# Conv, scan, attention and experts on one core: first scans with their C products on GpSimd, later openings by chunks, side work in halves

## The chip, the cores and the metric

The kernel runs on one core of a Trainium2 chip. The metric is the device time of one execution in microseconds. The engines are TensorE (PE), VectorE (DVE), ScalarE (ACT), GpSimd (POOL) and SyncE (SP), which here only issues DMAs.

## The reference, cut

There are 4 images of L = 4096 tokens with 128 channels, all in fp32. Each image goes through two layers. Layer 0 makes three selective scans of its tokens: forward, backward, and in 16 interleaved slices. Layer 1 is an attention with 16 heads of 8 features, a small feed-forward block, and 64 experts that each pool the tokens.

```python
# layer 0, for each of three orders of the tokens ("order" 0, 1, 2)
xz = in_proj_w @ norm(x)                      # 512 x L: 256 rows x, 256 rows z
u = silu(causal_conv1d(x, conv_w, conv_b))    # 4 taps
dt_raw, B, C = split(x_proj_w @ u)            # 8, 16 and 16 rows
delta = softplus(dt_w @ dt_raw + dt_b)        # 256 x L
h[d, n] = h[d, n] * exp(delta[d] * A[d, n]) + delta[d] * u[d] * B[n]    # over t
y[d] = sum_n h[d, n] * C[n] + D[d] * u[d]
out = out_proj_w @ ((y_f + y_b + y_s) * silu(z)) + x
# layer 1
q = ring(norm(out) + theta)                   # products of cosines, 16 heads x 8
ctx = softmax(q q^T / sqrt(8)) q              # 4096 x 4096 for each head and image
x1 = ln(norm(out) + w_comb @ ctx); h = relu(w1 @ z(x1)); x2 = ln(x1 + w2 @ h)
# experts: gate logits over tokens, best 8 of each, pooled tokens through two matrices, scattered back
```

## The kernel before

**Scan layout.** A scan step treats 8 channels x 16 states as rows: 128 partitions by T = 1024 tokens. A chunk (an order's 1024 tokens, 4 to an order) needs 32 steps, written as (order, c, k, j) with k in 0..7 and j in 0..3. An image has 3 x 4 x 32 = 384 steps. `Scans.of_image` is a generator that emits one step in two yields. `load` (L489) brings `delta` and `du` from DRAM, spread over 8 states each, for two steps at a time. `exp` (L503) makes dA = exp(delta * A) on ACT. `inputs` (L510) multiplies du by B on DVE. `step` scans on DVE (L519), copies the last column to `ends` on POOL (L521), calls `inputs` for the next step, and multiplies h by C on DVE (L524). `total` (L551) sums over the states with matmuls against `sel`. `out` (L567) adds D * u once for four steps and stores the result (L570, L576, L580) from POOL's queue. `product` (L544) makes `du` of a later chunk in parts between steps.

**Inputs.** `Inputs.pieces` yields the pieces that make the scans' inputs for all images: `norm`, `slices`, `of_chunk` (convolution as matmuls L387, silu L394, projections L401 and copy L404, L418, softplus L422, stores L370, L406, L407) and `gate` (silu of z, L351). They go through `flow`, which keeps two pieces in hand and steps them in turn, the second starting 10 yields after the first. Three PSUM tiles of 1024 columns are theirs.

**Stages.** An order of instructions written by hand sets all of this: each engine's queue gets its instructions in the order in which the generators yield. `Pace.run(share)` advances a chain of generators by a share of a step for each call.

1. First scans: image 0's 384 steps beside all images' inputs, 1.03 yields of the inputs for each yield of the scan.
2. `block.opening(0)`: tokens of image 0 (sum of the three orders' results, times silu(z), output projection, norm) and their rings q and v.
3. Loops over images 0, 1, 2. A loop has 1024 rounds of (j, qb, kc): 4 matmuls of scores (L924), two ACT exponentials of 128x1024 (L929, tile e), 4 matmuls of values into `acc` (L938). After each round, `beside(i)` advances the next image's scans and one step of other work: `after` of the image before (feed-forward), then `opening` of the next image, which starts when the next image's scans are done. What is left of the opening when the loop ends runs by itself before the next loop.
4. The loop over image 3. Its blocks of 512 queries are finished in turn, so that `after` of image 3 and the experts' pooling run beside it, 0.92 steps a round. A `yield PE` from `bank.take` marks a step that is about to put matmuls on PE; the side work has one PSUM bank.
5. The end: the last block's feed-forward, expert matrices, scatter.

In a round the order is scores of the next round, values of this one, then what stands beside it:

```python
            if i + 1 < len(rounds):
                scores(i + 1)
            values(i)
            if kc == NT - 1:
                sums(j, qb, i)          # acc copied by ACT, L947
            ...
            beside(i)
```

The side work's matmuls are `co` (L1041), `zt` (L1062), `h` (L1076), `fo` (L1087), `xT` (L1109), `lg` (L1119), `wt` (L1254), `pool` (L1265).

Of the kernel before, what the change touches and what calls it, by code (L numbers as in the profile page):

```python
# [16 lines left out]
P = 128  # L17
# [6 lines left out]
SLICES = 16  # L24
T = 1024
# [183 lines left out]

def early(b, order, c):  # L210

    return b == 0 or (b == 1 and order == 0 and c < 2)
# [15 lines left out]
class Inputs:  # L228
# [26 lines left out]
    def bank(self, name):  # L255
        while self.held == 3:
            yield WAIT
        self.held += 1
        return self.ps.tile([P, T], F32, tag="a", name=name)
# [4 lines left out]
    def pieces(self, images):  # L264

        for b in images:
            self.sz[b] = self.dram.tile([DI, L], F32, name=f"d_sz_{b}")
            yield self.norm(b)
            for order in range(3):
                if order == 2:  # L270
                    yield self.slices(b)
                for c in range(NC):
                    yield self.of_chunk(b, order, c)
                    third, at = divmod(order * NC + c, 3)
                    if at == 2:
                        yield self.gate(b, third)

    def norm(self, b):
# [10 lines left out]
        for g in range(NC):  # L289
            x_g = self.piece.tile([P, 8, C], F32, tag="x_g", bufs=2, name=f"x_{b}_{g}")  # L290
            nc.sync.dma_start(out=x_g, in_=xin[:, g * 8 : g * 8 + 8, :])
            yield
            ps = yield from self.bank(f"xt_{b}_{g}")
            for k in range(8):
                nc.tensor.transpose(ps[:, k * P : (k + 1) * P], x_g[:, k, :], self.ident)
            cut = xn[:, 3 + g * T : 3 + (g + 1) * T]
            nc.scalar.copy(cut, ps)
            self.leave()
            yield
            for k in range(2):  # L300
                nc.vector.bn_stats(stats[:, 2 * g + k, :], cut[:, k * 512 : (k + 1) * 512])
# [36 lines left out]
    def gate(self, b, g):  # L338
        nc, xn = self.nc, self.normed[b]
        s_g = self.piece.tile([P, 2, T], F32, tag="u", bufs=2, name=f"z_{b}_{g}")  # L340
        for m in range(2):
            ps = yield from self.bank(f"z_{b}_{g}_{m}")
            for i in range(T // 512):
                at = 3 + g * T + i * 512
                nc.tensor.matmul(
                    ps[:, i * 512 : (i + 1) * 512], self.w_z[:, m * P : (m + 1) * P], xn[:, at : at + 512],
                    start=True, stop=True,
                )
            yield
            yield  # L350
            nc.scalar.activation(s_g[:, m, :], ps, AF.Silu)  # L351
            self.leave()
        nc.gpsimd.dma_start(out=self.sz[b].rearrange("(m p) t -> p m t", p=P)[:, :, g * T : (g + 1) * T], in_=s_g)
# [3 lines left out]
    def of_chunk(self, b, order, c):  # L357
# [11 lines left out]
        def keep(name, t):  # L369
            nc.gpsimd.dma_start(out=made[name].rearrange("(m p) t -> p m t", p=P), in_=t)  # L370
# [11 lines left out]
        banks = []  # L382
        for m in range(2):
            ps = yield from self.bank(f"cv_{key}_{m}")
            for g, cut in enumerate(halves):
                for k in range(4):
                    nc.tensor.matmul(  # L387
                        ps[:, cut], w["conv"][:, k, m * P : (m + 1) * P], reads(k, g), start=(k == 0), stop=(k == 3)
                    )
                yield  # L390
            banks.append(ps)
        yield
        for m in range(2):
            nc.scalar.activation(u[:, m, :], banks[m], AF.Silu, bias=w["conv_b"][:, m : m + 1])  # L394
# [3 lines left out]
        ps = yield from self.bank(f"xd_{key}")  # L398
        for cut in halves:
            for m in range(2):  # L400
                nc.tensor.matmul(ps[:X_ROWS, cut], w["x"][:, m, :], u[:, m, cut], start=(m == 0), stop=(m == 1))  # L401
        yield
        xd = self.piece.tile([X_ROWS, T], F32, tag="xd", name=f"xds_{key}")
        nc.scalar.copy(xd, ps[:X_ROWS])  # L404
        self.leave()
        nc.gpsimd.dma_start(out=made["bc"][0], in_=xd[B_ROW : B_ROW + NS])  # L406
        nc.gpsimd.dma_start(out=made["bc"][1], in_=xd[C_ROW : C_ROW + NS])  # L407
        yield

        r = self.piece.tile([P, 2, T], F32, tag="r", bufs=2, name=f"r_{key}")  # L410
        banks = []
        for m in range(2):
            banks.append((yield from self.bank(f"dt_{key}_{m}")))
        for m in range(2):
# [1156 lines left out]
```

## Time and profile before

| | us |
|---|---|
| runs | 11714.78, 11721.87, 11722.49 |
| median | 11721.87 |
| the profiled execution, its own time | 11713.44 |
| its span, first to last instruction | 11711.7 |
| first scans (from the first scan's inputs to the last scan of image 0) | 97 to 1955 |
| opening of image 0 | 1955 to 2176 |
| loops over images 0, 1, 2 | 2176 to 4571, 4615 to 6978, 7021 to 9346 |
| loop over image 3 | 9348 to 11463 |
| end | 11463 to 11712 |

Busy time over the span: PE 10319 us (88%), ACT 10020 (86%), DVE 8551 (73%), POOL 3373 (29%). These are means over stages that differ, so they tell little; the stages have to be read one by one. In the profile a line such as L519 is the line of the kernel, a tile's name stands without its buffer number, and `out<-in` names what an instruction writes and reads. An idle time is put down to what ended it.

### The profile page before, as it was taken

To read this page: it belongs to the slowest core of one execution; us is meant where nothing else is said; L and a number is where in the kernel's file an instruction comes from. 1 tells how busy PE (TensorE), PEld (TensorE's weight loads), DVE (VectorE), ACT (ScalarE), POOL (GpSimd) and SP (SyncE) were. 2 spreads that over 40 slices of the span, in tenths; PEclk is the share of its full clock that TensorE was granted. 3 is DMA by queue.
4 is the path that set the end of the run, shared out by engine and by line. 5 is a ranking of instruction groups with operands and counts; after the bars stand their busy time and mean duration, and the time that the engine had idled before them with its cause. 6 is when DMAs were issued, how large, how long until landed. Compare 5 with 4: busy or idle time off the path is not lost.

```text
span 11711.7 us, 181745 instructions
## 1 busy us (share of the span) xinstructions
PE 10319.3 (88%) x68038; PEld 3430.9 (29%) x68038; DVE 8550.7 (73%) x8743; ACT 10019.7 (86%) x10604; POOL 3373.1 (29%) x4017
## 2 busy tenths in 40 slices
PE   6677674699999997999999979999999999999995
PEld 2222231222222232333333222333332223333323
DVE  7999998898988877998898879989887321101113
ACT  4565563699999997999999989999999999999992
POOL 5525362231323222324244223243341111000011
PEclk8888786799999998999999989999999999999997
DMA  6777777655565556665656566565555322222125
GB/s 186 219 222 209 212 209 204 174 152 154 150 155 147 145 161 173 158 157 147 156 140 154 150 176 168 152 153 142 150 138 137 120 93 67 75 70 76 59 73 187
DMA packets 835819, 1747.47 MB, mean 149 GB/s; under 512 B 141070, under 2 KB 373574, under 8 KB 834678
## 3 DMA queue, kind: packets, MB, share of 16 engines
q1 hardware_dynamic: 649438, 1318.65, 42.3%
q0 software_dynamic: 144000, 307.48, 8.5%
q10 hardware_dynamic: 41496, 109.71, 3.5%
q8 instruction: 534, 8.75, 0.3%
q14 instruction: 351, 2.88, 0.1%
HBM read 1379.76 MB, written 355.47 MB: 148 GB/s over the span
## 4 chain that ended last, share of the span: by engine, by line
PE 58%; DVE 13%; ACT 10%; issue 9%; DMA 8%; SPq 1%; POOL 0%; ACTq 0%; DVEq 0%; POOLq 0%
PE acc L938 33%; PE s L924 15%; ACT e L929 7%; DVE h L519 7%; PE y L551 4%; DMA delta<-d_delta 3%; DVE dB L510 2%; DMA du<-d_du 1%; PE fo L1087 1%; DVE du L510 1%; PE h L1076 1%; DMA y<-d_y 1%; PE cv L387 1%; DMA w<-in_L_ffn_weight_dram 1%; ACT dA L503 1%
## 5 line engine op out<-in xcount | busy, mean ns | idle before, releaser
L929 ACT ACTIVATE e<-s 128x1024 f32<-128x1024 f32 x8192 | 7777.3, 1102 | 357.9 <-PE s L924 313.0
L938 PE MATMUL acc<-e,val 128*32 128x512 f32 x32768 | 5676.3, 612 | 79.5 <-ACT av L947 78.7
L924 PE MATMUL s<-qm,key 32*128 32x512 f32 x16384 | 2784.7, 501 | 370.5 <-ACT e L929 310.5
L521 POOL COPY ends<-h 128x1 f32<-128x1 f32 x1152 | 1608.5, 1396 | 2597.6 <-DVE h L519 2590.9
L924 PEld LDWEIGHTS s<-qm,key 32*128 32x128 f32 x16384 | 1067.4, 183 | 3619.9 <-issue 1948.1
L938 PEld LDWEIGHTS acc<-e,val 128*32 128x32 f32 x32768 | 1028.4, 108 | 2009.7 <-issue 1015.4
L519 DVE TENSOR_TENSOR_SCAN h<-delta,ends,du 128x1024 f32<-128x1024 f32 x576 | 1353.5, 2350 | 86.3 <-ACT delta L503 77.1
L519 DVE TENSOR_TENSOR_SCAN h<-dA,ends,dB 128x1024 f32<-128x1024 f32 x576 | 1353.3, 2350 | 21.4 <-ACT dA L503 17.8
L503 ACT ACTIVATE dA<-delta,A 128x1024 f32<-128x1024 f32 x768 | 938.6, 1222 | 482.0 <-DMA delta<-d_delta 426.4
L510 DVE TENSOR_TENSOR dB<-du,B 128x1024 f32<-128x1024 f32 x768 | 931.8, 1213 | 549.8 <-PE y L551 370.1
L503 ACT ACTIVATE delta<-delta,A 128x1024 f32<-128x1024 f32 x768 | 938.9, 1222 | 75.3 <-PE y L551 68.4
L510 DVE TENSOR_TENSOR du<-du,B 128x1024 f32<-128x1024 f32 x768 | 925.6, 1205 | 28.7 <-DMA B<-d_bc 28.7
L524 DVE TENSOR_TENSOR dB<-h,C 128x1024 f32<-128x1024 f32 x768 | 939.6, 1223 | 0.0
L524 DVE TENSOR_TENSOR du<-h,C 128x1024 f32<-128x1024 f32 x768 | 939.4, 1223 | 0.1
L551 PE MATMUL y<-du,sel 128*32 128x256 f32 x6144 | 738.5, 404 | 184.1 <-DVE du L524 183.9
L551 PE MATMUL y<-dB,sel 128*32 128x256 f32 x6144 | 733.5, 400 | 91.6 <-DVE dB L524 40.9
L953 POOL DMA_DIRECT2D d_ctx<-av x512 | 260.7, 521 | 922.5 <-ACT av L947 912.7
L387 PE MATMUL cv<-xn,conv 128*128 128x512 f32 x1024 | 488.4, 632 | 20.0 <-DVE xn L322 20.0
L580 POOL DMA_DIRECT2D d_y<-o x512 | 329.6, 673 | 550.8 <-DVE o L567 489.9
L545 POOL DMA_DIRECT2D d_du<-x_delta x272 | 155.2, 571 | 1105.4 <-DVE x_delta L544 1029.2
L519 DVE TENSOR_TENSOR_SCAN h<-delta,du 128x1024 f32<-128x1024 f32 x192 | 439.2, 2287 | 13.1 <-ACT delta L503 7.1
L519 DVE TENSOR_TENSOR_SCAN h<-dA,dB 128x1024 f32<-128x1024 f32 x192 | 439.2, 2287 | 11.9 <-ACT dA L503 10.6
(245 smaller groups left out, 6450.8 us busy)
## 6 DMA issues: line engine op xcount, KB each, us to landing
delta<-d_delta SPq DMA_DIRECT2D x768, 512.0 KB
du<-d_du SPq DMA_DIRECT2D x576, 512.0 KB
du<-d_du ACTq DMA_DIRECT2D x192, 512.0 KB
key<-d_q SPq DMA_DIRECT2D x352, 256.0 KB
d_u<-u POOLq DMA_DIRECT2D x48, 1024.0 KB, 7.1
d_delta<-r POOLq DMA_DIRECT2D x48, 1024.0 KB, 6.5
B<-d_bc SPq DMA_DIRECT2D x96, 512.0 KB
C<-d_bc SPq DMA_DIRECT2D x96, 512.0 KB
```

What stands on the lines that cost most here:

```text
L387: nc.tensor.matmul(ps[:, cut], w["conv"][:, k, m * P : (m + 1) * P], reads(k, g), start=(k == 0), stop=(k == 3))
L503: nc.scalar.activation(tiles["delta", s], t, AF.Exp, scale=A)
L510: nc.vector.tensor_mul(tiles["du", s], du, spread[order, c, "B", j % 2])
L519: nc.vector.tensor_tensor_scan(h, dA, dB, first, ALU.mult, ALU.add)
L521: nc.gpsimd.tensor_copy(ends[order, c][:, at : at + 1], h[:, T - 1 :])
L524: nc.vector.tensor_mul(dB, h, spread[order, c, "C", j % 2])
L551: nc.tensor.matmul(y[32 * g : 32 * g + 32, : T // 4], self.sel[:, j // 2, :], hC[:, 256 * g : 256 * g + 256], start=(j == 0), stop=(j == 3),)
L580: nc.gpsimd.dma_start(out=to.rearrange("p (i j) -> p i j", i=SLICES)[:, :, at : at + n], in_=rows.rearrange("p (i j) -> p i j", i=SLICES),)
L924: nc.tensor.matmul(s_ps[:, k, :], keys[f"{i // 4}"][rows, cut].bitcast(F32R), queries[j, qb][rows, :].bitcast(F32R), start=True, stop=True,)
L929: nc.scalar.activation(e, s_ps, AF.Exp, scale=1.0 / math.sqrt(D))
L938: nc.tensor.matmul(accs[j, qb][32 * k : 32 * k + 32, :], v[:, k * VW : k * VW + 32], es[i][k // 2][:, k % 2, :], start=(kc == 0), stop=(kc ...
L953: nc.gpsimd.dma_start(out=self.context[b][h * D : h * D + D, cut], in_=av[32 * k : 32 * k + D, :])
```

## The change

**First scans.** Each `step` of image 0 (`alone`) multiplies h by C on POOL, into tiles of their own (hC, 5 of them), and DVE multiplies by B two steps ahead instead of one, always into a `dB` tile. `exp` writes dA to PSUM (two tiles of 1024 columns); the `h` of odd steps takes the buffers that dA had. Loads go out 4 steps ahead instead of 2. The sums' stores are kept for later and issued from SP. The inputs use PSUM tiles of 512 columns (three of them): every convolution, projection, silu and softplus is done by halves, silu one half at a time. The stores of the inputs go out from SP's queue instead of POOL's. The du products of the 14 early chunks (12 of image 0, 2 of image 1) move from DVE to POOL, two halves each, except the first chunk's. The inputs advance by 1.2 yields instead of 1.03.

**Later images.** Images 1 to 3 scan the orders as 1, 2, 0. Order 0's result stands in a DRAM tensor for each chunk. A block of `tokens` waits until the sums that it reads are stored, and the opening runs as soon as `after` is done, before the scans have ended. The scans aim at round 890 instead of 860.

**Loops.** In each round `beside(i)` comes before `values(i)`. In the last loop `acc` is copied by DVE, the matmul pieces zt, h, fo, xT and lg are cut in two by a `yield PE`, and side work goes by `Pace.turn(1.5, free)`: at most one PE step in a round, none in every third round up to round 830.

```diff
 def early(b, order, c):
-    return b == 0 or (b == 1 and order == 0 and c < 2)
+    return b == 0 or (b == 1 and order == orders(b)[0] and c < 2)
...
+        return self.ps.tile([P, 512], F32, tag="a", name=name)
...
         def keep(name, t):
-            nc.gpsimd.dma_start(out=made[name].rearrange("(m p) t -> p m t", p=P), in_=t)
+            nc.sync.dma_start(out=made[name].rearrange("(m p) t -> p m t", p=P), in_=t)
...
+                ps = yield from self.bank(f"cv_{key}_{m}_{g}")
                 for k in range(4):
                     nc.tensor.matmul(
+                        ps, w["conv"][:, k, m * P : (m + 1) * P], reads(k, g), start=(k == 0), stop=(k == 3)
                     )
                 yield
+                nc.scalar.activation(u[:, m, cut], ps, AF.Silu, bias=bias)
+                self.leave()
...
+            yield
+            for g, cut in enumerate(halves):
+                nc.scalar.activation(
+                    r[:, m, cut], banks[g], AF.Softplus, bias=w["dt_proj_b"][:, m : m + 1]
+                )
+                self.leave()
...
+            by = nc.vector if (b, order, c) == (0, orders(0)[0], 0) else nc.gpsimd
+            for m in range(2):
+                by.tensor_mul(u[:, m, :], r[:, m, :], u[:, m, :])
...
+            if alone:
+                tiles["delta", s] = self.ps.tile([P, T], F32, tag="dA", name=f"dA_{b}_{s}")
...
+            tag = "dA" if alone and j % 2 else "h"
+            h = self.deep.tile([P, T], F32, tag=tag, bufs=2, name=f"h_{b}_{s}")
             first = 0.0 if c == 0 else ends[order, c - 1][:, at : at + 1]
             nc.vector.tensor_tensor_scan(h, dA, dB, first, ALU.mult, ALU.add)
             if c < NC - 1:
                 nc.gpsimd.tensor_copy(ends[order, c][:, at : at + 1], h[:, T - 1 :])
+            if alone:
+                if s + 2 < n:
+                    inputs(s + 2)
+                tiles["du", s] = self.lone.tile([P, T], F32, tag="hC", bufs=5, name=f"hC_{b}_{s}")
+                nc.gpsimd.tensor_mul(tiles["du", s], h, spread[order, c, "C", j % 2])
+                return
...
+        c, part = divmod(g, T // 512)
+        while self.scans.stored[b] < min(8 * (2 * NC + c + 1) + 2, 8 * 3 * NC):
+            yield WAIT
...
-            nc.scalar.copy(av, accs.pop((j, qb)))
+            (nc.vector.tensor_copy if by_block else nc.scalar.copy)(av, accs.pop((j, qb)))
...
-            values(i)
-            if kc == NT - 1:
-                sums(j, qb, i)
...
             beside(i)
+            values(i)
+            if kc == NT - 1:
+                sums(j, qb, i)
...
                 for f in range(4):
+                    if f == 2:
+                        yield from self.pause()
...
+    def turn(self, share, free):
+        self.credit = min(self.credit + share, 3.0)
+        while self.credit >= 1 and not self.done and (free or self.then is not PE):
+            free = free and self.then is not PE
+            self.step()
...
-                others.run(1.03)
+                others.run(1.2)
...
-                following.run(min(1.3, max(0.5, left / max(1, 860 - i))))
-                other = last if not last.done else opens if left == 0.0 else None
-                if other is None:
+                following.run(min(1.3, max(0.5, left / max(1, 890 - i))))
+                other = opens if last.done else last
+                if other.done:
                     return
...
-        block.loop(nb - 1, lambda i: last.run(0.92), True)
+        block.loop(nb - 1, lambda i: last.turn(1.5, i % 3 > 0 or i > 830), True)
```

## The prediction

> **What bounds the kernel now.** I first cut the span at its stages (busy time by stretch; columns: length, then PE, PEld, DVE, ACT, POOL busy with counts, then granted clock, DMA share, GB/s).
>
> ```profile
> 97.00:1955.00 1858.00, 1319.65 (x5558) 504.57 (x5558) 1827.88 (x1331) 1082.85 (x935) 915.79 (x819) 0.82 0.74 214
> ...
> 2176.00:4571.00 2395.00, 2224.45 (x15726) 693.22 (x15726) 2058.77 (x1729) 2326.78 (x2495) 678.36 (x897) 0.98 0.59 153
> 4571.00:4615.00 44.00, 7.83 (x52) 3.39 (x50) 36.35 (x47) 6.74 (x8) 15.28 (x15) 0.62 0.74 222
> ...
> 9348.00:11463.00 2115.00, 2074.01 (x13534) 651.67 (x13534) 361.83 (x942) 1940.32 (x2110) 174.77 (x307) 0.99 0.24 73
> ```
>
> The first scans (384 steps in 1858 us, 4.84 each) are bound by DVE, busy 1828. The loops over images 0 to 2 (2395, 2363, 2325 us) are bound by ACT, 97% busy. Between them lie 44 and 43 us in which ACT does almost nothing. In the last loop ACT idles 175 of 2115 us.
>
> Next the timeline inside the first stage, DVE's and then POOL's (start, length):
>
> ```profile
> 1009.16 1.20 DVE L510 TENSOR_TENSOR du<-du,B 128x1024 f32<-128x1024 f32 x1
> 1010.28 1.22 DVE L524 TENSOR_TENSOR dB<-h,C 128x1024 f32<-128x1024 f32 x1
> 1011.41 2.35 DVE L519 TENSOR_TENSOR_SCAN h<-delta,ends,du 128x1024 f32<-128x1024 f32 x1
> 1013.68 1.20 DVE L510 TENSOR_TENSOR dB<-du,B 128x1024 f32<-128x1024 f32 x1
> ```
> ```profile
> 1009.31 2.23 POOL L521 COPY ends<-h 128x1 f32<-128x1 f32 x1 [5.20 <-DVE h L519]
> ```
>
> By starts a step costs DVE 1.12 (times B) + 1.13 (times C) + 2.27 (scan). POOL's copy of one column starts at 1009.31 and ends at 1011.54, just after the two products: it was locked out. The same shows on a POOL operation that takes 0.19 us undisturbed (minimum, median, maximum ns):
>
> ```profile
> L48 POOL TENSOR_TENSOR rs_x<-mv_x,eps x24: 195/2144/2158, 4754.5 to 6333.7; 128x4 f32<-128x4 f32 x24
> ```
>
> The long ones began under a scan of two SBUF tensors. ACT has 775 us left in this stage, but look at its table loads (groups by form, the stage's window):
>
> ```profile
> L503 ACT ACT_TABLE_LOAD x127 | 162.9, 1283 | 98.3 <-DMA delta<-d_delta 96.6
> ...
> L394 ACT ACT_TABLE_LOAD x47 | 60.3, 1283 | 0.8
> L422 ACT ACT_TABLE_LOAD x47 | 60.3, 1283 | 0.8
> ...
> L351 ACT ACT_TABLE_LOAD x32 | 41.1, 1283 | 0.6
> ```
>
> Last, the waits of 4571 to 4615, and ACT's of the last loop:
>
> ```profile
> ACT e L929 <- PE s L924: 18.2, 1, 18.2
> ...
> PE s L924 <- DMA key<-d_q: 15.2, 1, 15.2
> ```
> ```profile
> ACT e L929 <- PE s L924: 135.0, 188, 1.1
> ACT e L929 <- PE h L1076: 39.2, 60, 0.7
> ```
>
> The gap is the next image's opening, whose end the first keys await. In the last loop ACT waits for scores that stand behind side matmuls on PE.
>
> **What the Trainium skill says.** "SBUF — State Buffer", Who interferes with whom: a DVE instruction with two SBUF inputs and a GpSimd instruction that reads SBUF lock each other out whole; one with at most one SBUF input doesn't. The trace agrees: under scans L48 takes about 2.15 us, but under L1079 (one PSUM tensor and a column from SBUF) 192 to 197 ns. "GPSIMD Engine Reference", Elementwise: a product of 2048 fp32 takes 4497 ns on GpSimd against 2293 on DVE. DVE's 128x2048 product takes 2302 here; the trace has no GpSimd product of that kind. "ScalarE: Activation LUTs", What ACT_TABLE_LOAD costs: 1283 ns and a drain of some 1380. The trace has the 1283, but only 17 ns before and 12 after it; with the lost overlap (about 0.1) I price a switch at 1.41.
>
> **Part 1, the first scans.** The products with C go to POOL: 384 x 1.13 = 434 us off DVE. The scan reads dA from PSUM; that operand should cost DVE nothing (a 128x256 sum with a PSUM operand, L776, takes 417 ns; L544 from SBUF 420), at worst 0.1 a step. POOL's product I take at 2.25 (half of the page's 4497); bounds are 1.13 (DVE's own) and, an estimate, 3.4 (half as much again). The lock then sets the chain: after a scan DVE multiplies by B (1.12) while POOL waits; then POOL copies (0.04 + 0.19) and multiplies (2.25) while the next scan runs (2.27), and the next B product waits for POOL. That makes 3.6 a step. At every fourth step the sum L567 (0.5) makes it 3.9, on average 3.67; x384 = 1409. The du products of 13 early chunks also go to POOL: 26 x 2.25 = 59. Sum 1468, 3.82 a step. POOL is freed of the stage's stores (about 510 issues, 312 us busy), which go to SP. SP then issues some 870 DMAs at about 0.54 = 470 us, and each store waits there for ACT or DVE with the next loads queued behind it; since loads go out four steps ahead (15 us) I cost that at nothing. The same DMA traffic in 1680 us is a share of 0.74 x 1858/1680 = 0.82, which the trace reaches in places.
>
> ACT is what may eat the gain. In 512-column pieces each silu half comes after a yield of its own and each softplus pair too, so exponentials fall between them. Following the yields of the two interleaved chunks and the scan step by step, before gives 255 loads (the page has 127+48+48+32) and after gives 460: 139 before silu of u, 61 softplus, 31 gates, 229 exponentials. ACT's work by spacing: exponentials 384 x 1.05 = 403, silu and softplus 384 halves x 0.585 (1.012 less 512 x 0.833 ns) = 225, copies 128 x 0.47 = 60, gates 64 x 0.51 = 33, slices 30, loads 460 x 1.41 = 649: 1400 us, nearly all in the first 353 steps (at pace 1.2 the inputs end there), 3.87 a step. That is the chain's own pace, and it is uneven: stretches with silus need 5 to 6.5, and with two dA buffers ACT can be only one step ahead. Adding up the larger of chain (3.82) and ACT's work gives about 1570 if four steps may balance, 1690 if none may. PE's waits for POOL's products and ACT's for half a convolution speak for the upper end: I take 1680, **a gain of 180**; bounds +30 (slower) and -290. The input banks shrink from three of 1024 columns to three of 512, so PE can lead ACT by three halves only; that wait is in the choice of the upper end.
>
> **Part 2, loops 0 to 2.** With order 0 scanned last, opening blocks start at 74 of 96 stored sums, and only two blocks and the second half's rings are left when the scans end near round 900 of 1024. At about a step a round that is 60 rounds: the opening ends inside the loop. The gaps (87 us) go, less the 9 us of exponentials done there and a few: -75. Values after the side work lets PE fill its wait for the last e of a round; PE-caused idle is 39, 39 and 56 us per loop: -30. DVE (86% and 87% busy in the first two loops) gets crowded while opening and scans overlap: +15. **-90**, bounds 0 and -190. Costed at nothing: the swapped order and order 0's sums in a tensor per chunk (the same bytes), the pace of 890 in place of 860 (124 rounds are left behind it), and the wait for stored sums at the head of an opening block, behind which nothing is queued, since it only skips its turn.
>
> **Part 3, the last loop.** Rounds without side matmuls start 1.815 us apart. By what PE did between, the others cost extra: 60 with fo 1.05 each, 60 with h 0.84, 30 with co 0.64, 48 with wt or pool 1.03, 15 with zt 0.47, 14 each with lg 0.97 and xT 0.57: 211 us. That is more than the pieces themselves (fo and h 0.86), for they stand between the values, which end late, and the next scores. After, 404 pieces of at most 0.43 stand between scores and values, where PE waits for e anyway, one in a round and none in every third. In 1.81 us PE needs 0.44 for scores and 0.9 for values, so a half nearly fits; I take 0.2 each (bounds 0 and 0.35): 81, a gain of 130. The 31 accumulator copies that cost a round 0.47 move to a DVE that is 17% busy, but PE still waits for them: -7. By the yields the side work now ends near round 951 instead of 13 steps after the loop: -12. **-150**, bounds -70 and -220.
>
> **Sum.** The profiled execution took 11713.4 (span 11711.7, 1.7 around it): 11713 - 180 - 90 - 150 = 11293. The median of the runs is 8 above that execution: **11300**.
>
> **Rivals.** (a) ACT takes the whole gain of part 1: for it the 205 added loads (289 us), against it ACT's 775 idle us; 11722 - 240 = 11480. (b) The loops give little, because DVE saturates in the overlap and a PE half costs its switch again: 0 and -70 for parts 2 and 3; 11722 - 180 - 70 = 11470. (c) Slower: the scan still locks POOL out, because its first state is a column in SBUF. Then nothing overlaps: 1.12 + 2.27 + 0.23 + 2.25 = 5.87 a step, 384 x 5.87 + 59 = 2313, +455; 11722 + 455 - 240 = 11940. It decides from 5.47 us a step (4.84 + 240/384). Against it: L1079 and L567 also read such columns, and POOL ran under them undisturbed. (d) The PSUM decays don't buy a faster stage because POOL's product takes over 3.4: part 1 is 0, as in (a).
>
> **Numbers.** The forecast 0.69, (a) with (d) 0.17, (b) 0.08, slower by (c) or a like lock 0.05, nothing measurable 0.01. A measurement of this kernel tells 0.2% (23 us) from no change. Range 11130 (stage 1 at 1570, and 60 more from the loops) to 11530 (past (a) and (b), with 50 for what both can lose besides); it leaves out (c) and the best corner.
>
> **What would show it.** Right: first stage 1570 to 1750 us, 4.1 to 4.6 a step, POOL above DVE in busy share, about 460 table loads, POOL's products near 2.3; no stretch over 10 us without e between the loops; last loop under 2000 and no e waiting for h. Wrong: scans or B products of 3 us and more (a lock that I misread), POOL's product far from 2.3, a first stage near 1850 with ACT over 85% busy, or the opening still running when a loop ends.

## The result

The changed kernel takes 11545.6 us (median of 4 runs, 11534.4 to 11551.4) against 11721.3 before: a ratio of 0.985, with a 95% interval of 0.9833 to 0.9867. It is faster by 176 us, or 1.5%, which is clear of the noise; the forecast was 420, and the time lies 16 us above the range. The profiled execution spans 11538.0 us. I cut it at the same places as before: first scan to last scan of image 0, then the loops from first to last exponential e.

| us | before | predicted change | after | change |
|---|---|---|---|---|
| up to the first scan | 101.6 | 0 | 113.8 | +12 |
| first scans (384 steps) | 1834.7 | -180 | 1828.2 | **-7** |
| to the first e | 239.3 | 0 | 243.9 | +5 |
| loops 0 to 2 | 7083.9 | -15 | 7063.9 | -20 |
| the two gaps between them | 86.9 | -75 | 6.3 | -81 |
| last loop | 2114.8 | -138 | 2030.8 | **-84** |
| after it | 248.9 | -12 | 249.4 | 0 |

The sum of the last column is the 174 us between the two spans (the remaining stretch before the last loop is 1.6 us in both). Part 2 came as worked out. Part 1 gave nothing, part 3 some 60%. A single execution of the loops over images 0 to 2 tells little below some 10 us: in the runs below that leave them alone they take 7060 to 7083 us, 7071 on average.

Busy time by stretch of the kernel after; columns as before (length, PE, PEld, DVE, ACT, POOL busy with counts, then clock, DMA share, GB/s):

```profile
110.00:1945.00 1835.00, 1421.40 (x5527) 556.60 (x5531) 1432.67 (x926) 1376.44 (x1409) 1339.81 (x714) 0.82 0.75 213
2186.00:4563.00 2377.00, 2128.59 (x15690) 631.62 (x15690) 2043.14 (x1740) 2321.89 (x2490) 682.93 (x907) 0.98 0.60 156
4563.00:4564.20 1.20, 1.20 (x10) 0.29 (x6) 1.20 (x2) 0.48 (x2) 0.00 (x0) 1.00 0.93 252
9258.00:11289.00 2031.00, 1961.69 (x13688) 630.76 (x13690) 393.39 (x995) 1924.51 (x2078) 177.11 (x314) 0.98 0.25 76
```

In the first row DVE lost 395 us of work and the stretch is nearly as long as it was. Four engines are now busy for 73 to 78% each and none of them is full: the stage changed from one that DVE filled into one in which every engine waits. The third row is all that is left of the first gap.

A step of the first scans in the timeline of the kernel after (start, length, engine, line):

```profile
999.12 2.35 DVE L542 TENSOR_TENSOR_SCAN h<-dA,ends,dB 128x1024 f32<-128x1024 f32 x1 [7.19 <-issue]
...
1001.38 1.20 DVE L532 TENSOR_TENSOR dB<-du,B 128x1024 f32<-128x1024 f32 x1
1001.53 1.09 POOL L544 COPY ends<-h 128x1 f32<-128x1 f32 x1 [7.25 <-DVE h L542]
...
1002.58 2.35 POOL L549 TENSOR_TENSOR hC<-h,C 128x1024 f32<-128x1024 f32 x1
...
1003.55 2.35 DVE L542 TENSOR_TENSOR_SCAN h<-dA,ends,dB 128x1024 f32<-128x1024 f32 x1 [0.97 <-POOL ends L544]
```

POOL's copy waits out the product with B, its product takes 2.35 us and runs beside the scan: the mechanism is the one predicted, and a scan that reads dA from PSUM costs DVE no more than before (2.35). The first line shows the trouble: DVE stood idle for 7.19 us before that scan. The profile puts this down to "issue", that is, to nothing that it could name; but the exponential dA that the scan reads ended at 999.03, 0.09 us before it. Over the stage the distance from scan to scan is about 3.4 us or less in a quarter of the steps, 4.4 in the middle one, and over 6.8 in one of ten; before, the middle half lay between 4.51 and 4.90.

ACT's table loads in the stage (groups by form; count, busy us, mean ns, idle before):

```profile
L525 ACT ACT_TABLE_LOAD x228 | 292.5, 1283 | 23.8 <-DMA delta<-d_delta 11.5 <-DMA du<-d_du 4.4 <-DMA d_y<-o 3.7
L400 ACT ACT_TABLE_LOAD x136 | 174.5, 1283 | 69.7 <-PE cv L396 49.2 <-issue 16.4 <-DMA d_du<-u 2.0
...
L427 ACT ACT_TABLE_LOAD x60 | 77.0, 1283 | 3.1 <-issue 2.1
...
L358 ACT ACT_TABLE_LOAD x31 | 39.8, 1283 | 0.6
```

They are 455 in this window and 461 in all, where 460 were counted from the turns.

### The profile page after: what moved, and what is told of

It reads as the page before. It is cut to its first block, busy times and chain, and to the rows that moved or that the text cites. A ratio compares the mean times of both kernels' runs of the same rounds, so it can differ in the third digit from the quotient of the medians.

```text
span 11538.0 us, 182909 instructions
## 1 busy us (share of the span) xinstructions
PE 10009.7 (87%) x68358; PEld 3314.4 (29%) x68358; DVE 8174.7 (71%) x8379; ACT 10305.7 (89%) x11065; POOL 3770.4 (33%) x3917
## 4 chain that ended last, share of the span: by engine, by line
PE 34%; ACT 23%; issue 14%; DVE 7%; DMA 6%; POOL 1%; SPq 1%; ACTq 0%; DVEq 0%; POOLq 0%
PE acc L992 20%; ACT e L983 20%; PE s L978 9%; DVE h L542 2%; DMA du<-d_du 1%; DMA delta<-d_delta 1%; ACT dA L525 1%; PE fo L1149 1%; ACT delta L525 1%; PE h L1136 1%; DMA w<-in_L_ffn_weight_dram 1%; DVE dB L532 1%; PE y L580 1%; DMA y<-d_y 0%; DVE du L553 0%
## 5 line engine op out<-in xcount | busy, mean ns | idle before, releaser
L992 PE MATMUL acc<-e,val 128*32 128x512 f32 x32768 | 5250.0, 616 | 105.5 <-ACT av L1001 91.6
L544 POOL COPY ends<-h 128x1 f32<-128x1 f32 x1152 | 1264.9, 1099 | 2501.6 <-DVE h L542 2486.2
L542 DVE TENSOR_TENSOR_SCAN h<-dA,ends,dB 128x1024 f32<-128x1024 f32 x720 | 1687.6, 2344 | 337.2 <-issue 205.7
L532 DVE TENSOR_TENSOR dB<-du,B 128x1024 f32<-128x1024 f32 x960 | 1197.0, 1247 | 408.0 <-PE y L580 221.2
L542 DVE TENSOR_TENSOR_SCAN h<-delta,ends,du 128x1024 f32<-128x1024 f32 x432 | 1012.1, 2343 | 132.1 <-ACT delta L525 65.4
L549 POOL TENSOR_TENSOR hC<-h,C 128x1024 f32<-128x1024 f32 x384 | 976.8, 2544 | 146.8 <-DVE h L542 73.0
L553 DVE TENSOR_TENSOR du<-h,C 128x1024 f32<-128x1024 f32 x576 | 700.9, 1217 | 0.1
L553 DVE TENSOR_TENSOR dB<-h,C 128x1024 f32<-128x1024 f32 x576 | 700.8, 1217 | 0.0
L580 PE MATMUL y<-dB,sel 128*32 128x256 f32 x4608 | 376.7, 399 | 9.9 <-DVE xT L1176 6.2
L580 PE MATMUL y<-hC,sel 128*32 128x256 f32 x3072 | 255.5, 467 | 144.7 <-DVE o L596 139.6
```

Of the source, the lines that this page charges most:

```text
L532: nc.vector.tensor_mul(tiles["du", s], du, spread[order, c, "B", j % 2])
L542: nc.vector.tensor_tensor_scan(h, dA, dB, first, ALU.mult, ALU.add)
L544: nc.gpsimd.tensor_copy(ends[order, c][:, at : at + 1], h[:, T - 1 :])
L549: nc.gpsimd.tensor_mul(tiles["du", s], h, spread[order, c, "C", j % 2])
L553: nc.vector.tensor_mul(dB, h, spread[order, c, "C", j % 2])
L580: nc.tensor.matmul(y[32 * g : 32 * g + 32, : T // 4], self.sel[:, j // 2, :], hC[:, 256 * g : 256 * g + 256], start=(j == 0), stop=(j == 3),)
```

## What DVE waits for: the first stage

**Where the idle time is.** For every step I took from the trace whether DVE was idle before the scan (by more than 0.15 us) and whether the exponential dA had only just ended. Before the change this happened at the very first scan alone. After it, 193 of 384 scans start late behind their exponential, and DVE idles 337.5 us there. The stretch that ends in the 7.19 us, on PE and ACT:

```profile
987.89 1.28 ACT L400 ACT_TABLE_LOAD   x1 [3.50 <-PE cv L396]
...
988.74 10.57 PE L396 MATMUL cv<-xn,conv 128*128 128x512 f32 x24
...
992.48 0.69 ACT L400 ACTIVATE u<-cv,conv_b 128x512 f32<-128x512 f32 x1 [2.61 <-PE cv L396]
995.91 0.69 ACT L400 ACTIVATE u<-cv,conv_b 128x512 f32<-128x512 f32 x1 [2.75 <-PE cv L396]
...
996.62 1.28 ACT L525 ACT_TABLE_LOAD   x1
997.91 1.12 ACT L525 ACTIVATE dA<-delta,A 128x1024 f32<-128x1024 f32 x1
```

ACT takes its work in order. It waits for half a convolution, does its silu, waits for the next half; PE needs 3.43 us for each. Then it loads the exponential's table, and only then comes the exponential that the scan has been waiting for since about 992. Two PSUM buffers of dA let ACT be one step ahead, so little of this can be done earlier. (A third buffer was not tried.) In the 193 late steps, between the moment when the buffer came free and the start of the exponential, ACT spent 600 us on table loads (377 of them for the exponential itself), and some 170 in waits for convolutions, 125 in silus and 120 in softplus.

**Theory.** Three things stand between the chain (3.6 us a step) and the stage: table loads, dense convolutions on PE with ACT waiting between the halves, and what PE has to wait for in its order. **Rivals:** the loads are all of it; or they are nothing and POOL's part is simply too slow. In the table, stage is first to last scan of image 0, gap from there to the first e; these come from one profile of each kernel. The totals of the changed kernel and of e3 are medians of 4 executions, the others are a single one. The runs e4 and e8 further down leave the stage alone and show it at 1829.5 and 1833.3, so some 5 us in it mean nothing.

| run | stage | gap | last loop | total |
|---|---|---|---|---|
| after | 1828 | 244 | 2031 | 11545.6 |
| e1 no table loads | 1697 | 245 | 2029 | 11407.7 |
| e2 decays in SBUF | 2213 | 246 | 2032 | 11936.5 |
| e3 silus in pairs | 1807 | 245 | 2032 | 11529.5 |
| e5 C products on DVE | 1937 | 247 | 2035 | 11666.0 |
| e6 sum one step earlier | 1777 | 242 | 2032 | 11493.5 |
| e12 two taps | 1736 | 244 | 2031 | 11456.8 |
| e7 = e1 + two taps | 1590 | 246 | 2032 | 11313.5 |
| e9 = e7 + e6 | 1561 | 244 | 2038 | 11278.0 |
| e13 = e9 + new loads of x | 1487 | 273 | 2035 | 11224.4 |

**e1, no table loads.** Silu and softplus are replaced by exponentials, so these two functions are left out.

```diff
-   nc.scalar.activation(u[:, m, cut], ps, AF.Silu, bias=bias)
+   nc.scalar.activation(u[:, m, cut], ps, AF.Exp, bias=bias)
```
The same for z and for r.

> The changed kernel with silu and softplus of the scans' inputs computed as exponentials, so that the first scans need no table load (the scans then work on other numbers; every shape and every order of instructions is kept). The changed kernel needs 1828 us from the first scan to the last one of image 0. Theory A (the exponential that the next scan needs stands on ACT behind table loads, with only one step of lead): the 460 loads become one or two, and the stage falls to the chain of B product, column copy and POOL's C product, 3.6 to 3.9 us a step: 1400 to 1520 us, the run some 300 to 400 us under the changed kernel. Theory B (PE and ACT wait for each other over the three half banks, whatever the tables do): the stage stays over 1720. Theory C (the shared port between DVE and POOL sets the pace): the stage stays over 1750.

The stage falls by 131 us to 1697, between the theories. The idle time behind late exponentials falls from 337.5 to 149.6 us, but ACT's waits for convolutions rise. Waits between 110 and 1700 us (total, times, longest), first of the kernel after, then of e1:

```profile
ACT u L400 <- PE cv L396: 93.3, 50, 4.7
```
```profile
ACT u L400 <- PE cv L396: 435.7, 159, 12.1
...
PE y L580 <- DVE o L596: 69.4, 21, 7.3
```

Freed of 584 us of loads (455 x 1.283), ACT waits 342 us longer for PE before its silus (a part of this wait stood before the loads themselves until now, 49.2 us in the stage). So all loads together are worth 131, and PE's share is next.

**e2, decays in SBUF.** The exponentials of image 0 go to SBUF as before, so that h has its two buffers of before again, and all else stays.

```diff
-   if alone:
-       tiles["delta", s] = self.ps.tile([P, T], F32, tag="dA", name=f"dA_{b}_{s}")
-   elif j % 2 == 0:
+   if j % 2 == 0:
        tiles["delta", s] = self.deep.tile([P, T], F32, tag="dA", bufs=2, name=f"dA_{b}_{s}")
    ...
-   tag = "dA" if alone and j % 2 else "h"
-   h = self.deep.tile([P, T], F32, tag=tag, bufs=2, name=f"h_{b}_{s}")
+   h = self.deep.tile([P, T], F32, tag="h", bufs=2, name=f"h_{b}_{s}")
```

> The changed kernel with dA written to SBUF as in the kernel before (even steps in a buffer, odd steps in place of delta), C products still on POOL. The scan then has two SBUF inputs. If a scan of two SBUF inputs locks POOL's product out for its whole length, nothing overlaps: 1.12 + 2.27 + 0.23 + 2.3 = 5.9 us a step, the stage 2250 to 2320 us, 400 to 500 over the changed kernel. If POOL's product only shares bandwidth with the scan, or is not locked at all, ACT's longer lead (up to three steps) makes the stage the same or faster, 1450 to 1830.

Timeline of this run, DVE and then POOL:

```profile
1004.48 2.28 DVE L539 TENSOR_TENSOR_SCAN h<-dA,dB 128x1024 f32<-128x1024 f32 x1
1006.68 3.30 DVE L530 TENSOR_TENSOR dB<-du,B 128x1024 f32<-128x1024 f32 x1
...
1010.29 4.21 DVE L539 TENSOR_TENSOR_SCAN h<-delta,dB 128x1024 f32<-128x1024 f32 x1
```
```profile
1004.55 4.34 POOL L546 TENSOR_TENSOR hC<-h,C 128x1024 f32<-128x1024 f32 x1
1008.84 1.18 POOL L541 COPY ends<-h 128x1 f32<-128x1 f32 x1
1009.98 2.38 POOL L546 TENSOR_TENSOR hC<-h,C 128x1024 f32<-128x1024 f32 x1
```

The product that begins at 1004.55 has stood under the scan of 1004.48, and the product with B behind it; the scan at 1010.29 has stood under a product. The stage is 2213 us, 5.76 a step; rival (c) of the prediction worked out 2313 (5.87 a step and the du products), 5% more. That is the lock which the Trainium skill states ("SBUF — State Buffer", Who interferes with whom), and here it is worth 384 us. Without the decays in PSUM the change would be slower than the kernel before (11936.5 us). The timeline of the kernel after shows that a first state read from an SBUF column does not bring the lock back: POOL's product from 1002.58 to 1004.93 runs under the scan that starts at 1003.55.

**e3, silus in pairs.** Both halves of a convolution are made before their two silus.

```diff
+   banks.append(ps)
    yield
+   for cut, ps in zip(halves, banks):
        nc.scalar.activation(u[:, m, cut], ps, AF.Silu, bias=bias)
```

> The changed kernel with the two silu halves of a row block issued one after the other, when both convolution halves are made (two banks held). Counting the yields, the first stage has 370 table loads instead of 460. Theory A: 90 loads of 1.41 us less on ACT, most of them ahead of an exponential; the stage falls by 50 to 120 us (1710 to 1780), the run likewise. Theory B: two of three banks are held longer, PE waits more, and the stage is the same or up to 60 us slower.

371 loads instead of 461, and the stage is 21 us shorter (ratio to before 0.9836, 0.9819 to 0.9852). A load saved is worth 0.23 us here and 0.28 in e1 (131/460): far less than its 1.28. That many of them lie beside a wait would explain it; this is my reading, not a test.

**e5, C products on DVE.**

```diff
-   nc.gpsimd.tensor_mul(tiles["du", s], h, spread[order, c, "C", j % 2])
+   nc.vector.tensor_mul(tiles["du", s], h, spread[order, c, "C", j % 2])
```

> The products with C of image 0 go back to DVE, everything else stays (dA in PSUM, one y bank, 461 table loads). DVE then has 384 x (1.12 + 1.13 + 2.27) plus sums and the wait at each step. Theory A (the exponential's lead is the limit): in this kernel a step is 4.52 us or more, so ACT has 1.2 us more per step to hide its loads in, and the exponential is seldom late; the first stage then takes 1790 to 1860 us, that is no more than now (1828): POOL's part brought nothing that the loads did not take back. Theory B (POOL's product is worth its 434 us less the loads): the stage takes 2000 us or more. The other stages stay within 10 us.

1937 lies between the theories. It splits part 1 in two: with the products on DVE the stage is 102 us **longer** than before the change (1937 against 1835). This is what the rest of part 1 costs there (half banks with 461 loads, one y bank, two dA buffers, a faster pace of the inputs). DVE is as busy as before (1821 us), and its waits make up the difference: 66.0 us for late exponentials, 26.7 for the next image behind ACT, 20.3 for PE to free a product's buffer. POOL's products take back 109. Part 1 is the difference, -7.

**e6, the sum with D one step earlier.** The single y bank is read by DVE's sum; it is issued at turn 3 of a group instead of at turn 0 of the next.

```diff
-   if turn == 0 and alone and s >= 8:
-       finish(s - 5, y)
+   if turn == 3 and alone:
+       finish(s - 4, y)
```

> In the first stage the sum with D (y to o) is issued one step earlier (at turn 3 for the group just finished), so the single y bank comes free a step sooner. Theory A (loads and dense convolutions before the exponential): the wait of PE for that bank (67 us of PE idle named 'PE y <- DVE o') shrinks, the stage moves by less than 25 us. Rival (the single y bank, which stands before the convolutions in PE's order, is what delays them): the stage falls by 40 us or more, to below 1790.

1777: the rival was right. PE's wait for this sum between 110 and 1700 us, after and then in e6:

```profile
PE y L580 <- DVE o L596: 60.7, 20, 12.6
```
```profile
PE y L580 <- DVE o L596: 18.0, 7, 6.8
```

It falls by 43 us and the stage by 51. The bank stands ahead of the convolutions in PE's order, and one step of it is worth these 51 us. The same edit also frees the tile u that the sum reads a step earlier, for which SP's loads wait; but ACT waits for DMAs in the first stage for no more than 34 us in the kernel after and 45 in e6, and PE waits for x as long without the edit as with it (90.9 and 89.0), so the gain does not come from there. Before the change there were two such banks.

**e12 and e7, two of four taps**, alone and with e1. The other two taps are left out of the computation.

```diff
-   for k in range(4):
+   for k in range(2, 4):
```

> Only the convolution is cut to two of its four taps; the table loads stay. Theory A (loads and convolutions delay the same exponentials and hide each other in part): the stage falls by less than with the loads away (107 us), by 30 to 80, to 1750 to 1800. Rival (the two add): it falls by 100 or more.

> The silus and softplus are exponentials (as in the run without table loads) and the convolution takes two of its four taps, so this kernel leaves both out. Without loads the stage was 1697. Theory A (PE's dense stretches of convolution, 24 halves of 3.44 us per image order, are what remains): each half takes 1.72 us, ACT's waits for the convolution fall from 436 to under 250 us and the stage falls to 1480 to 1600. Rival (POOL's product with its copy, 2.75 us a step, and the single y bank set the rest): the stage stays above 1640.

Half of the convolution is worth 92 us with the loads (between theory and rival of e12) and 107 without (as theory A of e7 had it: ACT's wait for convolutions falls from 435.7 to 183.7). That is nearly the same, so the two hardly hide each other, against what I expected. In e7 the idle time behind late exponentials is down to 26.8 us, and PE's wait for the y bank is next (waits, 110 to 1700):

```profile
PE y L580 <- DVE o L596: 285.2, 60, 15.3
```

**e9, the three together.**

> Silu and softplus as exponentials, two of the four taps (both left out of the computation), and the sum with D a step earlier. With the first two the stage was 1590, and PE then waited 285 us for the one y bank. Theory A (the three together are what stood between the predicted chain and the stage): the stage falls to the chain's own pace, 384 x 3.82 = 1467 plus a little, 1450 to 1540. Rival (something else, such as POOL's products locked or the DMAs at a share of 0.86, holds it): it stays above 1550.

1561, 21 above the theory's upper end and on the rival's side of 1550: something else held it. In nine of twelve stretches of 32 steps it runs at 112 to 132 us (3.5 to 4.1 a step), but three take 164, 148 and 148. These are the stretches in which the next image comes in. In the kernel after they are 176, 167 and 173. There PE and DVE wait for the image (kernel after, 110 to 1700 us):

```profile
PE xt L302 <- DMA x<-in_x_dram: 90.9, 12, 17.9
```
```profile
DVE stats L307 <- ACT xn L304: 37.3, 16, 7.6
```

The transposes are issued one turn after the load of x and PE waits in order; DVE's statistics wait for them with the next scan behind.

**e13, new loads of x**, on top of e9: tiles of four blocks in two buffers, loaded four turns before their transposes, the statistics a tile later, and the pace at 1.25.

```diff
+   x_h = bring(0)
+   for h, cut in enumerate(cuts):
+       for _ in range(4):
+           yield
        ...
+       if h + 1 < len(cuts):
+           x_h = bring(h + 1)
        nc.scalar.copy(cut, ps)
+       if h:
+           nc.vector.bn_stats(stats[:, h - 1, :], cuts[h - 1])
```

> As the run with three things taken away (silu and softplus as exponentials and two of four taps left out of the computation; early sum), and the next image's x is loaded in tiles of 4 blocks in two buffers, each four turns of the side work before its transposes, with its statistics a tile later. That run took 1561, at 3.69 us a step in nine of its twelve stretches of 32 steps, but 164, 148 and 148 us in the three where an image is brought in. Theory (x arrives late, PE and behind it ACT and DVE wait in order): these three fall to about 128, the stage to 1490 to 1520. Rival (the statistics and the scaling of the image themselves, about 11 us of DVE per image, and the DMAs at 0.88): the stage stays above 1540.

The three stretches fall to 124, 120 and 125 and the stage to 1487, though 29 us of input work now lie behind the last scan. The first scan also starts 4 us earlier (109.4), a third of the 12 us that the change lost ahead of it. The edit has several parts (the earlier loads, the later statistics, the pace), which were not run apart. The timeline of this run shows the predicted chain with nothing in its way, DVE and then POOL:

```profile
1004.83 2.34 DVE L551 TENSOR_TENSOR_SCAN h<-dA,ends,dB 128x1024 f32<-128x1024 f32 x1
1007.09 1.20 DVE L541 TENSOR_TENSOR dB<-du,B 128x1024 f32<-128x1024 f32 x1
1008.20 2.34 DVE L551 TENSOR_TENSOR_SCAN h<-dA,ends,dB 128x1024 f32<-128x1024 f32 x1
...
1018.33 0.47 DVE L605 SCALAR_TENSOR_TENSOR o<-us,D,y 128x256 f32<-128x256 f32 x1
```
```profile
1007.31 3.19 POOL L558 TENSOR_TENSOR hC<-h,C 128x1024 f32<-128x1024 f32 x1 [0.58 <-DVE h L551]
```

3.37 us from scan to scan (1.12 + 2.25, in a chunk without copies of ends), 3.77 with the sum. With the copies the middle steps of e13 take 3.43 and 3.91. By these medians (3.38 and 3.77 where nothing is copied) 384 steps need about 1356 us, and with 26 du products of 2.35 us at most 1417: the chain of 1467 us had the right links and was some 50 us too long. Four things lie on top of it. The prediction had the loads as work of ACT, and the others at nothing or in a word ("the upper end"). Taken away in this order they are 131 (loads), 107 (half the convolution), 29 (sum) and 74 (x, 45 net of the longer gap), together 341 us. That e13 comes within 20 us of 1467 is partly luck: some 70 us of other waits still stand in its 1487. What each thing is worth depends on the order in which they go; in the changed kernel itself the loads are worth 131, half the convolution 92 and the sum 51.

**e15 and e17, the new loads of x in the changed kernel**, with the pace at 1.25 and at 1.32.

> The changed kernel with only the new loading of x. Its three stretches with an image took 176, 167 and 173 us against some 147 in the others. Theory: they fall by 10 to 20 each, the stage from 1828 to 1770 to 1800. Rival (the table loads of the chunks that follow the image set these stretches anyway): the stage moves by less than 15.

> As the changed kernel with the new loading of x, with the pace of the inputs at 1.32 in place of 1.25: by the count of turns they then end at step 371 instead of 17 turns after the last scan. Theory: the gap before loop 0 goes back from 283 to about 245, the stage stays within 15 of 1781, total 11490 to 11510. Rival (the higher pace packs the inputs' work and the stage gives back what the gap gains): total above 11525.

e15: stage 1781 as expected, but a gap of 283, total 11538.8; nothing is won. e17: gap 242 again, but the stage goes to 1856, total 11567.3: the rival. So an earlier x brought something only where ACT and PE had time to spare (e13 against e9). My reading, which no run tests: with the loads in place the time in which x is late holds no silus, and without it they are only packed closer elsewhere.

## The loops

**e8, side work after the values in loops 0 to 2.**

```diff
-   beside(i)
+   if by_block:
+       beside(i)
    values(i)
    ...
+   if not by_block:
+       beside(i)
```

> In the loops over images 0 to 2 the side work is put after the values again, as before the change; the last loop keeps the new order. If that order is worth what I priced (30 us): loops 0 to 2 together take 7094 instead of 7064 us. Rival (it is worth nothing there since the exponentials bound these loops): they stay within 10 us of 7064. First stage and last loop within 10 us of now.

7086 us against 7064. The runs that leave these loops alone give 7060 to 7083, so the order is worth between 3 and 26 of the 30 us that I priced, 15 against their mean; a single profile settles no more, and next to nothing is not ruled out.

**The last loop.** By the distance between the first e of successive rounds, an undisturbed round takes 1.825 us (before 1.810); over 1024 rounds this is some 15 us, for which I have no cause. Rounds with halves cost little: fo 22.9 us in 188 rounds, wt 12.9, pool 9.0, co 7.3, zt 5.8, lg 4.2, xT 1.5, h 0.5, together 64 where I had 81. The copy of the accumulator costs 1.6 us in rounds that are not delayed otherwise, against 13.7. But 19 rounds without a table load lose 1.3 us or more each, 71 us in all (one 7.8). In 15 of them (63 us) a co, h, xT or wt is issued in the turn after its input was begun, and PE, in order, holds the scores behind it. At 1.5 steps a round these follow one another faster than at 0.92, and the lag (the turns left between a producer and the matmuls that read it) is 0 in this loop. ACT's wait after, and then in e4 (waits of the last loop):

```profile
ACT e L983 <- PE s L978: 96.5, 80, 7.6
```

**e4, a waiting turn.**

```diff
-   block.loop(nb - 1, lambda i: last.turn(1.5, i % 3 > 0 or i > 830), True)
+   block.lag = 1
+   block.loop(nb - 1, lambda i: last.turn(1.5, i % 4 > 0 or i > 830), True)
+   block.lag = 0
```

> The changed kernel with lag 1 in the last loop (one more yield between a producer on DVE and the matmuls that read it) and PE steps left out in every fourth round instead of every third, so that the side work still ends inside the loop. Theory: of the last loop's 2031 us some 65 are rounds of 3 us and more in which a side matmul was issued before its input was there and PE, in order, held up the scores. With the lag most of them go: the last loop takes 1970 to 1995 us. Rival (the side halves themselves and the copy of acc by DVE are the cost): the last loop stays at 2015 to 2045. The first stage stays at 1828.

```profile
ACT e L983 <- PE s L978: 46.3, 62, 7.2
```

The loop takes 1979, 52 less, and 1977 was predicted; the long rounds fall to 7 with 27 us, of which two with wt (13 us) stay as they were. Total 11502.3 (ratio to before 0.9814, 0.9799 to 0.9828). So nearly all that was missing from part 3 is matmuls that came before their inputs. The edit also moves the free rounds from every third to every fourth; the two were not run apart, but the ACT wait that falls is the one for scores.

## A faster version

> Three edits that each helped alone: the sum with D a step earlier (-51 in the first stage), silus in pairs (-21 there), and a waiting turn before side matmuls of the last loop with every fourth round free of them (-52 there). If they add: first stage 1756, last loop 1979, total 11545 - 51 - 21 - 43 = 11430, ratio to before 0.975. If pairs and early sum meet the same waits: 11450.

e3, e4 and e6 in one: stage 1760, last loop 1979, 11423.4 us (median of 4), ratio 0.9746 (0.9730 to 0.9762). They add.

e11 puts a yield between the second and third tap, and the pace at 1.45:

```diff
    for k in range(4):
+       if k == 2:
+           yield
```

> As the run before with a yield between the second and third tap of each half convolution and the pace of the inputs at 1.45 in place of 1.2, so that PE gets at most 1.7 us of convolution at a time. Theory A (dense convolutions on PE delay exponentials and the sums' y bank): the stage falls by 20 to 60 more, total 11370 to 11410. Rival (only the total of PE's and ACT's work in a stretch counts): within 15 us of the run before, or slower, as the higher pace packs the table loads closer.

Stage 1718, **11394.1 us**, ratio 0.9722 (0.9708 to 0.9737): as the theory had it, with 413 loads instead of 371. Shorter stretches of PE and the higher pace together are worth more than the 42 loads cost. This is the fastest version that I ran with the whole computation in it, 152 us below the changed kernel.

> The fastest kernel so far (early sum, silus in pairs, split convolutions, last loop with a waiting turn) with the new loading of x and the pace of the inputs at 1.5. Theory: another 20 to 50 us, 11345 to 11375, ratio 0.968 to 0.971. Rival: within 15 us of 11394.

> As the run meant as the fastest, whose inputs were left with 81 turns after the last scan (a gap of 343 us before loop 0), with the pace at 1.65: they end at step 374. Theory: the gap goes back to about 245 and the stage rises by at most 30 from 1653, total 11325 to 11355, ratio 0.967 to 0.969. Rival (the packed inputs cost the stage what the gap gains): total above 11385.

e14 and e16 add the new loads of x to e11. Stage and gap are 1653 + 343 in the one and 1757 + 240 in the other, the same sum, against 1718 + 244 in e11: 11420.4 and 11410.6 us. Both miss what was expected, by the same trade of stage against gap as in e15 and e17.

## Why the prediction failed, point by point

- **Part 1, the chain:** right in its links, some 50 us too long. An undisturbed step takes 3.43 us and 3.91 with the sum (estimated 3.6 and 3.9; 3.37 and 3.77 where there is no copy), POOL's product 2.35 (estimated 2.25 from half of the figure in the Trainium skill, "GPSIMD Engine Reference", Elementwise), no price for dA in PSUM, 461 loads for 460. Rival (c) was priced within 5%, and its reason fell as argued. The longer queue on SP, costed at nothing, held too: ACT waits 34 us for DMAs in the first stage.
- **Part 1, the sum:** wrong, the step that failed. "1690 if none may balance" was taken as the upper end of the stage, and I took 1680; it took 1828. The sum adds, step by step, the larger of DVE's chain and ACT's own work, as if ACT began each step's work at once. ACT, one step ahead at most, spends part of that time waiting for PE's halves, and PE waits for the y bank and for x. I named the wait for convolutions and for half banks, and gave it no size ("in the choice of the upper end"); for the single y bank I had no term. In the changed kernel half of the convolution is worth 92 us and one step of the y bank 51, together 143 of the 148 us that are missing; that these two add was not run. The sign that I had given for rival (a) came by half: the stage is near 1850, but ACT is busy for 75% and not for over 85%. So ACT's waits and not its work alone ate the gain. A table load counts for less than its price: 289 us of ACT for the 205 added ones, while taking all 460 away brings 131. That the loads could eat POOL's gain was seen, as rival (a), with 0.17. The bounds of this part (+30 and -290) held the -7.
- **Part 2:** right. Gaps -81 for -75; loops -20 for -15 (-13 against the mean of the runs that leave them alone; values after side work 3 to 26 of 30).
- **Part 3:** the halves cost less than I took (64 for 81), the accumulator's copies won 12 for 7. Missing was a term: what a faster pace of side work without lag does to matmuls whose inputs are not there, 63 of the 71 us in long rounds; 52 came back in e4. The -12 for side work behind the loop did not come (249.4 for 248.9), though that work now ends inside the loop. The traces show another path there: the last block's own `co`, whose input goes through DRAM, begins 20.5 us behind the last e before the change and 26.0 after it, and the side work stood beside that wait.
- **The range:** its end at 11530 held rival (a) or rival (b), with 50 us more for what both can lose. Part 1 at -7 and part 3 at -84 came together, with 17 us ahead of and behind the first stage that no part had.

## To carry to other kernels

When the bottleneck engine is relieved, look for the engine whose queue is only one buffer ahead and add up what it waits for as well as what it does: here the stage became a sum of waits, and the second-busiest engine did not set it. Giving PSUM banks to one use (two of dA) takes them from others (input banks, the second y bank), and each that became single needs a price. When side matmuls are run at a faster pace, a fixed number of turns between an input and its use is a shorter time, so the number of turns has to grow.

## What the runs showed of the hardware

- The row of a POOL operation that is locked out holds that time as well: in e2 a product of 2.35 us shows as 4.34, in e13 as 3.19 where it stood under the product with B. Such a row must be read beside DVE's.
- With half of the convolution gone, PE's granted clock in the first stage is lower, not higher: 0.77 at 1043 us of PE busy in the 1490 between 110 and 1600 us (e12), 0.83 at 1196 in the kernel after. A convolution matmul (on xn) takes 710 ns in e12, against 641. So leaving out half of the taps takes away less than half of the convolution's time, and the 92 and 107 us hold with this lower clock.
- The DMA engines took a share of 0.88 and 255 GB/s between 110 and 1600 us in e9 (0.75 and 218 after), and ACT waited for delta 154.6 us in all there; loads four steps ahead then no longer always came in time.
